# Turning half of the attention probabilities by a DRAM round trip and VectorE instead of TensorE

## The chip, the cores and the metric

The kernel runs on one core of one Trainium2 chip, in one launch. The metric is the device time of that launch in microseconds (us). Before the change the median of three runs is 933.17 us (932.65 to 934.37).

## The reference, cut to what matters

One "macaron" block over a sequence of 2048 tokens with 1024 features: half a feed-forward layer, an attention layer, and the other half of the feed-forward layer, each added to its input.

```python
x = x + 0.5 * ffn(layernorm(x))
x = x + attention(layernorm(x))
x = x + 0.5 * ffn(layernorm(x))
```

The attention works in blocks of 128 tokens. A convolution over three tokens gives q, k and v (256 features each), and these are projected to 16 heads of 64. The part around the change is this, for each block `b` and head `h`:

```python
scores = einsum('bqhe,bkhe->bhqk', qh * scale, kh)
scores = where(causal, scores, -1e9)
p = softmax(scores, axis=-1)
o = einsum('bhqk,bkhe->bqhe', p, vh)
o = einsum('bqhe,hed->bqd', o, wo) + bo
out = o @ proj_w + proj_b
```

TensorE contracts over partitions. The scores come out with the queries on the partitions, and the product with `vh` contracts over the keys. So each 128 x 128 matrix `p` has to be turned in between. There are 16 blocks and 16 heads, 256 such matrices.

## The kernel before

The first feed-forward layer, the convolution (done as a fast convolution of eight products, line 585) and the second feed-forward layer (main products at line 311) are not touched. The change lies in the attention, from about 418 us to 785 us of the profile.

**Turns.** The tokens are split into 4 groups of 512 (4 blocks), numbered g = 0 to 3. The heads are taken two at a time (a "head pair" hp, its two heads j = 0 and 1), and two head pairs make one turn, r = 0 to 3. So there are 16 turns, i = 4 g + r, from 0 to 15. One turn deals with four tiles of probabilities, each 128 queries x 4 blocks x 128 keys (128 x 512 fp32, 256 KB), in a pool of four buffers: the copy that fills a tile in one turn has to wait until the same tile of the turn before has been read.

**TensorE's order is written out by hand** (`turn`, L1227, inside `manual_schedule`). In turn i TensorE does:

- `stage_qk` of turn i (pq, L870), the q and k projections
- `stage_wo` of turn i - 2 (acc, L1133)
- `stage_transpose` of turn i - 1 (pt, L1103): 16 transposes of 128 x 128, four to a tile
- `stage_scores` of turn i (sc, L1056)
- `stage_values` of turn i - 1 (ao, L1116), first for its first head pair, then for its second
- in turns with r = 0, i > 0, `stage_v` (pv, L870); in turns with r = 1, g > 0, `stage_proj` of the group before (pp, L1196). In turn 1, `stage_v` of group 0 stands ahead of the transposes.

So turns with r = 2 and 3 are short and turns with r = 0 and 1 are long, and a tile's softmax has the time from the scores of its turn to the transposes of the next. After turn 15 comes a hand-written tail, which mixes the end of the attention with the start of the second feed-forward layer (`Second`, L371).

**The softmax of a turn** (`stage_scores`, L1048): ScalarE copies the four score tiles from PSUM (L1065, kept in program order), GpSimd masks each (L1070), VectorE takes the row maxima (L1081), ScalarE does 16 exponentials with their sums (L1086), all after the last copy, and VectorE inverts the sums (L1093) and scales the tile (L1094, the "division"). `stage_transpose` then has TensorE turn a tile into PSUM, and ScalarE (j = 0, L1106) or VectorE (j = 1, L1108) copy it out as `pT`.

**The order on the other engines** is that of a planner, which sorts by priority, and is fixed when the program is built. Every engine's queue is worked off in order. That holds for the queue of SyncE (SP), which issues nearly all loads and stores, and for GpSimd's (POOL), which issues the accumulating DMAs between its other work: an instruction that waits holds up all that stand behind it.

**What else stands in these queues**, and is named later:

- `tokens_of` (L896): q and k of a later group, `x<-qkv`, four loads of 256 KB on SP, with their sums on GpSimd and VectorE (L851 to L854)
- `signs` (L1212): weights of the second feed-forward layer, `raw`, 512 KB each on SP, turned into signs by ScalarE (L1215)
- `load_residual` (L1146): the residual rows, `xr<-x` (L1149), four loads of 512 KB on SP, and on GpSimd's queue four accumulating DMAs that add `proj_b` to them (L1150), each waiting for its load
- `row_statistics` (L1154): in turns with r = 1 and 2, ScalarE's normalized rows `xp` (L1174) and their stores by quarters, `xq<-xp` (L1184), 16 of 128 KB for each group
- in the tail, `Second.load` (L378): `xl<-xq`, 512 KB each on SP (L380), and `Second.transpose` (L382), where VectorE turns them in 32 x 32 blocks (STREAM_TRANSPOSE, L387).

In the tail the load of `xl` for the first row tile, its two VectorE transposes and the four accumulating DMAs of the last group stand ahead of the maxima and masks of turn 15 in their queues, before the change and after it.

Of the kernel before, what the change touches and what calls it, by code (L numbers as in the profile page):

```python
# [9 lines left out]
F32 = mybir.dt.float32  # L10
# [3 lines left out]
ALU = mybir.AluOpType  # L14
AX = mybir.AxisListType
PSUM = bass.MemoryType.PSUM

P = 128
NB = 512
# [5 lines left out]
def kernel(  # L25
# [22 lines left out]
    nc = tc.nc  # L48
# [10 lines left out]
    BPG = NB // P  # L59
    NH2 = D // NB  # L60
    QC = 32
    QSCALE = 1.0 / (DH**0.5)

    def pool(stack, name, bufs, **kw):
        return stack.enter_context(tc.tile_pool(name=name, bufs=bufs, reuse_waits="tile", **kw))
# [4 lines left out]
    spill = pool(ctx, "spill", 1, space=DRAM)  # L70
# [4 lines left out]
    def bank(kind, shape, name):  # L75
        return banks[kind].tile(shape, F32, name=name, tag=kind)
# [26 lines left out]
    def pin(ins):  # L103

        return tc.keep_in_program_order(ins)
# [878 lines left out]
    with ExitStack() as ph:  # L984
        ow = pool(ph, "ow", 1)
        ap4 = pool(ph, "ap4", 4)
# [8 lines left out]
        prs, pTs, oTs, accs, qks, ended, stored, exps, maxima, masked, turned, divided = ({} for _ in range(12))  # L995
# [49 lines left out]
        def held(ins):  # L1045
            return tc.issue_after(ins.ins) if ins else ExitStack()

        def stage_scores(g, r, mask_behind=None, maxima_behind=None):  # L1048
            ps = []
            for hp, kind in zip((2 * r, 2 * r + 1), ("mm", "tr")):  # L1050
                qh, kh = qks.pop((g, hp))

                sc = [bank(kind, [P, BPG, P], f"sc_{g}_{hp}_{j}") for j in range(2)]
                for b in range(BPG):
                    for j in range(2):
                        nc.tensor.matmul(  # L1056
                            sc[j][:, b, :],
                            lhsT=qh[ts(j, DH), ts(b, P)],
                            rhs=kh[ts(j, DH), ts(b, P)],
                            start=True,  # L1060
                            stop=True,
                        )
                prs[g, hp] = [ap4.tile([P, BPG, P], F32, name=f"p_{g}_{hp}_{j}", tag="p") for j in range(2)]
                for p, acc in zip(prs[g, hp], sc):
                    copied = pin(nc.scalar.copy(p, acc)).ins  # L1065
                    ps.append(p)

            for n, p in enumerate(ps):
                with held(mask_behind):
                    masked[g, r] = nc.gpsimd.affine_select(  # L1070
                        out=p,
                        in_=p,
                        pattern=[[0, BPG], [-1, P]],
                        compare_op=ALU.is_ge,
                        fill=NEG_INF,
                        base=0,
                        channel_multiplier=1,
                    )
                nmax = small.tile([P, BPG], F32, name=f"anm_{g}_{r}_{n}", tag="anmax")
                with held(maxima_behind):  # L1080
                    ins = nc.vector.tensor_reduce(nmax, p, AX.X, ALU.max, negate=True)  # L1081
                maxima.setdefault((g, r), ins)
                asum = small.tile([P, BPG], F32, name=f"asum_{g}_{r}_{n}", tag="asum")
                with tc.issue_after(copied):
                    for b in range(BPG):
                        exps[g, r] = nc.scalar.activation(  # L1086
                            p[:, b, :],
                            p[:, b, :],
                            AF.Exp,
                            bias=nmax[:, b : b + 1],  # L1090
                            accum_out=asum[:, b : b + 1],
                        )
                nc.vector.reciprocal(asum, asum)  # L1093
                divided[g, r] = nc.vector.tensor_tensor(  # L1094
                    p, p, asum.unsqueeze(2).broadcast_to([P, BPG, P]), ALU.mult
                )

        def stage_transpose(g, hp, kind):
            pTs[g, hp] = []
            for j, p in enumerate(prs.pop((g, hp))):  # L1100
                pt = bank(kind, [P, BPG, P], f"pt_{g}_{hp}_{j}")
                for b in range(BPG):
                    nc.tensor.transpose(pt[:, b, :], p[:, b, :], ident)  # L1103
                pT = ap4.tile([P, BPG, P], F32, name=f"pT_{g}_{hp}_{j}", tag="pT")
                if j == 0:
                    nc.scalar.copy(pT, pt)  # L1106
                else:
                    turned[g, hp] = nc.vector.tensor_copy(pT, pt)  # L1108
                pTs[g, hp].append(pT)
# [108 lines left out]
        pairs = [(g, r) for g in range(NG) for r in range(NP)]  # L1218
# [8 lines left out]
        def turn(g, r, values):  # L1227
# [13 lines left out]
            if i == 1:  # L1241
                stage_v(0)
            two(stage_wo, i - 2)
            two(stage_transpose, i - 1, "sm", "tr")
            stage_scores(g, r)
            if values:
                two(stage_values, i - 1)
# [15 lines left out]
        with tc.manual_schedule(engines={mybir.EngineType.PE}):  # L1263
# [7 lines left out]
            g, r = pairs[-1]  # L1271
# [16 lines left out]
            for t in range(2):  # L1288
                load_rows2(t)
            two(stage_wo, LAST - 3)  # L1290
            two(stage_transpose, LAST - 2, "sm", "tr")
            with tc.issue_after(turned[g, NHP - 3].ins), tc.high_priority(offset=400):
                ffn.transpose(0)
            ffn.load(2)
            stage_scores(g, r, stored[g], ffn.turned)
            with tc.issue_after(masked[g, r].ins):
                for t in range(2):
# [3 lines left out]
            two(stage_wo, LAST - 2)  # L1301
            ffn.gate(0)
            stage_transpose(g, NHP - 2, "sm")
            with tc.issue_after(divided[g, r].ins):
                ffn.transpose(1)
# [75 lines left out]
```

## Time and profile before

| | |
|---|---|
| median of the three runs | 933.17 us |
| the profiled execution's own time | 932.75 us |
| its span (first to last instruction) | 930.9 us |
| TensorE (PE) busy | 908.7 us, 98% of the span |
| VectorE (DVE) busy | 673.3 us, 72% |
| ScalarE (ACT) busy | 451.0 us, 48% |
| GpSimd (POOL) busy | 234.8 us, 25% |
| PE transposes of p (pt, L1103) | 256, from 446.5 to 761.6 us |
| from the first score copy (L1065) of turns 4, 5, 6 and 7 to that of the next turn | 28.00, 28.99, 16.57, 15.85 us |

"Busy" does not say that an engine bounds a stage: matmuls are pipelined, and shares are averages. What sets the time is read from the chain of work that ended last and from the timelines of the single turns. A time line gives start and duration in us from the start of the span, engine, source line, operation, output and inputs, number of instructions, and in brackets the idle time before and what ended it. SPq is SyncE's queue of DMA issues. The first copies of turns 4 to 8 start at 496.84, 524.84, 553.83, 570.40 and 586.25 us.

### The profile page before, as it was taken

The page shows a single profiled execution, that of the slowest core. Times are in us where ns is not written, and L with a number is a line of the kernel's source. Part 1 is how long each engine was busy: PE and PEld are TensorE (multiplying, and loading weights), DVE is VectorE, ACT ScalarE, POOL GpSimd, SP SyncE. Part 2 cuts the span into 40 slices and gives each one's busy share as a digit, 9 for nine tenths or more (in the row PEclk, how much of TensorE's full clock was granted, in tenths as well). Part 3 has the DMA queues.
Part 4 walks back from the last instruction along what each step waited for, and adds up shares of the span by engine and source line. Part 5 has one row for each costly group of instructions (what it writes and reads, how often), then busy time and mean ns, then how long its engine had stood idle before and what let it go on. Part 6 is the DMA issues. An engine that isn't in the chain of part 4 may idle for free.

```text
span 930.9 us, 14379 instructions
## 1 busy us (share of the span) xinstructions
PE 908.7 (98%) x5112; PEld 647.9 (70%) x5112; DVE 673.3 (72%) x1353; ACT 451.0 (48%) x1231; POOL 234.8 (25%) x331
## 2 busy tenths in 40 slices
PE   6999999999999999999999999999999999999997
PEld 4778888886666666666775677667765765777775
DVE  5889887689978786657786668576757566866663
ACT  5676666431111111117787758666766752423230
POOL 2554454320001011101141123112412222443341
PEclk9999999999999999999999999999999999999999
DMA  9776663499576765445460149015702593997853
GB/s 350 172 197 191 183 192 137 153 297 348 178 223 176 202 189 128 89 160 181 148 139 10 46 147 283 25 47 168 193 1 92 189 263 130 313 271 217 246 159 113
DMA packets 51063, 161.64 MB, mean 174 GB/s; under 512 B 6376, under 2 KB 15592, under 8 KB 49072
## 3 DMA queue, kind: packets, MB, share of 16 engines
q1 hardware_dynamic: 39568, 114.69, 35.0%
q0 software_dynamic: 10688, 38.02, 20.9%
q10 hardware_dynamic: 736, 8.02, 2.3%
q8 instruction: 40, 0.66, 0.3%
q14 instruction: 31, 0.25, 0.1%
HBM read 97.69 MB, written 46.24 MB: 155 GB/s over the span
## 4 chain that ended last, share of the span: by engine, by line
PE 81%; DVE 6%; ACT 4%; DMA 3%; issue 3%; POOL 2%; SPq 0%; POOLq 0%; ACTq 0%; DVEq 0%
PE cv L585 23%; PE pm_f L311 20%; PE pq L870 8%; PE pp L1196 6%; PE pv L870 5%; PE acc L1133 4%; PE sc L1056 3%; PE ao L1116 3%; PE pt L1103 3%; DMA x<-in_x_dram 2%; PE lgp_f L228 2%; PE is_f L272 1%; ACT p L1086 1%; PE tr_f L220 1%; DVE st_f L167 1%
## 5 line engine op out<-in xcount | busy, mean ns | idle before, releaser
L311 PE MATMUL pm_f<-sw,y_f 128*128 128x512 f32 x1024 | 258.1, 403 | 0.6 <-ACT y_f L285 0.4
L311 PEld LDWEIGHTS pm_f<-sw,y_f 128*128 128x128 f32 x1024 | 187.0, 190 | 41.9 <-ACT y_f L285 0.8
L585 PE MATMUL cv<-v,u 128*128 128x342 f32 x576 | 166.0, 450 | 0.0
L585 PEld LDWEIGHTS cv<-v,u 128*128 128x128 f32 x576 | 109.0, 189 | 56.8
L286 POOL TENSOR_TENSOR y_f<-xnT_f,y_f 128x512 fp32r<-128x512 f32 x63 | 79.9, 1283 | 111.4 <-ACT y_f L285 111.4
L1086 ACT ACTIVATE p<-p,anm 128x128 f32<-128x128 f32 x256 | 99.9, 400 | 0.4 <-DVE anm L1081 0.4
L1070 POOL TENSOR_SCALAR_AFFINE_SELECT p<-p 128x512 f32<-128x512 f32 x64 | 39.3, 654 | 220.6 <-ACT p L1065 220.6
L602 ACT ACTIVATE m<-cv 128x342 f32<-128x342 f32 x42 | 19.2, 457 | 156.2 <-PE cv L585 154.1
L323 DVE TENSOR_TENSOR pm_f<-pm_f,os_f 128x512 f32<-128x512 f32 x64 | 44.7, 698 | 52.7 <-PE pm_f L311 52.4
L1081 DVE TENSOR_REDUCE anm<-p 128x4 f32<-128x512 f32 x64 | 40.2, 679 | 25.9 <-POOL p L1070 25.6
L585 PE MATMUL cv<-v,g 128*128 128x342 f32 (+2 forms) x224 | 57.1, 415 | 0.9 <-DVE v L507 0.9
L1133 PE MATMUL acc<-oT,wo_sb 128*128 128x512 f32 x128 | 57.9, 594 | 0.0
L1196 PE MATMUL pp<-pw_sb,o2T 128*128 128x512 f32 x128 | 56.6, 597 | 0.3 <-DVE xr L1204 0.3
L585 PEld LDWEIGHTS cv<-v,g 128*128 128x128 f32 x224 | 39.7, 190 | 17.6 <-DVE v L507 1.3
L1086 ACT ACTIVATION_READ_ACCUMULATOR p<-p,anm 128x1 f32 x256 | 51.0, 199 | 0.0
L1108 DVE COPY pT<-pt 128x512 f32<-128x512 f32 x32 | 22.1, 691 | 38.4 <-PE pt L1103 38.3
L297 ACT ACTIVATE os_f<-po_f 128x512 f32<-128x512 f32 x64 | 34.8, 595 | 24.3 <-PE is_f L272 14.1
L1094 DVE TENSOR_TENSOR p<-p,asum 128x512 f32<-128x512 f32 x64 | 44.9, 701 | 1.3
L1196 PEld LDWEIGHTS pp<-pw_sb,o2T 128*128 128x128 f32 x128 | 23.7, 190 | 30.1 <-issue 25.0
L573 DVE SCALAR_TENSOR_TENSOR u<-g,u 128x1024 f32<-128x1024 f32 x18 | 22.0, 1224 | 29.0 <-PE cv L585 13.2
L285 ACT CAST y_f<-xnT_f 128x512 fp32r<-128x512 f32 x64 | 37.5, 625 | 11.2 <-DVE xnT_f L283 11.2
L283 DVE TENSOR_TENSOR xnT_f<-xnT_f,is_f 128x512 f32<-128x512 f32 x64 | 40.9, 679 | 2.3 <-PE is_f L272 2.3
(190 smaller groups left out, 1645.5 us busy)
## 6 DMA issues: line engine op xcount, KB each, us to landing
g<-in_conv_w_dram SPq DMA_DIRECT2D x28, 512.0 KB, 4.9
u<-in_conv_w_dram POOLq DMA_DIRECT2D x24, 512.0 KB, 6.2
x<-in_x_dram SPq DMA_DIRECT2D x16, 512.0 KB, 4.6
raw<-in_weight_t_dram SPq DMA_DIRECT2D x16, 512.0 KB, 8.8
x<-hbias POOLq DMA_DIRECT2D x16, 512.0 KB, 5.5
x<-x SPq DMA_DIRECT2D x16, 512.0 KB, 4.2
xr<-x SPq DMA_DIRECT2D x16, 512.0 KB, 5.2
xr<-in_proj_b_dram POOLq DMA_DIRECT2D x16, 512.0 KB, 9.1
```

Source lines behind the costliest of these rows:

```text
L283: self.scaled = nc.vector.tensor_tensor(y, y, sc, ALU.mult)
L286: self.lowered = lows[h].tensor_tensor(yl, y, yh.bitcast(F32), ALU.subtract)
L311: ins = nc.tensor.matmul(pms[h], lhsT=y[:, n, c, :], rhs=self.sw[:, c, ts(h, NB)], start=(c == 0 and n == 0), stop=(c == DC - 1 and n == 1),)
L323: nc.vector.tensor_tensor(pms[h], pms[h], o, ALU.mult)
L585: nc.tensor.matmul(accs[w, k][:, lo:hi], lhsT=uk[:, c, :], rhs=V[k][:, c, lo:hi], start=(c == 0), stop=(c == DC - 1),)
L870: nc.tensor.matmul(leave.sums[sums], lhsT=rows[a][:, u, :], rhs=cols[b], start=n in (0, 1, 3), stop=True, skip_group_check=True,)
L1070: masked[g, r] = nc.gpsimd.affine_select(out=p, in_=p, pattern=[[0, BPG], [-1, P]], compare_op=ALU.is_ge, fill=NEG_INF, base=0, channel_mu ...
L1081: ins = nc.vector.tensor_reduce(nmax, p, AX.X, ALU.max, negate=True)
L1086: exps[g, r] = nc.scalar.activation(p[:, b, :], p[:, b, :], AF.Exp, bias=nmax[:, b : b + 1], accum_out=asum[:, b : b + 1],)
L1094: divided[g, r] = nc.vector.tensor_tensor(p, p, asum.unsqueeze(2).broadcast_to([P, BPG, P]), ALU.mult)
L1133: nc.tensor.matmul(accs[g][m], lhsT=wo_sb[:, hp, ts(m, P)], rhs=oT, start=(hp == 0), stop=(hp == NHP - 1),)
L1196: nc.tensor.matmul(pp, lhsT=o2T[:, m, ts(b, P)], rhs=pw_sb[:, m, ts(h, NB)], start=(m == 0), stop=(m == WC - 1),)
```

## The change

For every turn but the last, the tiles of the second head (j = 1) of both head pairs no longer go through TensorE, 30 tiles of the 64. Their scores are copied and kept with the keys in quarters, (quarter, block, key in the quarter). They take the lead in the softmax. After its division such a tile is stored to DRAM in four pieces, one for each quarter of the partitions, so that the quarter of the queries and the quarter of the keys change places, and is loaded back into the same tile. Then VectorE turns it in 32 x 32 blocks straight into `pT`. The planner may put the transposes only behind the last division of their turn. The tiles with j = 0, and all of turn 15, are as before.

```diff
+        def by_quarters(p):
+            return p.rearrange("p q (b k) -> p q b k", b=BPG)
+
+        def exchange(p, name):
+            there = spill.tile([P, NB], F32, name=name)
+            to = there.rearrange("(q b) c -> b q c", q=4)
+            for k in range(4):
+                nc.sync.dma_start(out=to[:, :, ts(k, P)], in_=p[ts(k, QC)])
+            nc.sync.dma_start(out=p, in_=there.rearrange("p (q c) -> p q c", q=4))
...
+            turned_on_vector = (g, r) != pairs[-1]
...
-                for p, acc in zip(prs[g, hp], sc):
+                for j in (1, 0) if turned_on_vector else (0, 1):
+                    p, acc = prs[g, hp][j], sc[j]
+                    quarters_of = turned_on_vector and j == 1
+                    if quarters_of:
+                        p, acc = by_quarters(p), acc.rearrange("p b (q k) -> p q b k", q=4)
                     copied = pin(nc.scalar.copy(p, acc)).ins
-                    ps.append(p)
-
-            for n, p in enumerate(ps):
+                    ps.append((quarters_of, hp, p))
+
+            for n, (quarters_of, hp, p) in enumerate(sorted(ps, key=lambda x: -x[0])):
+                if quarters_of:
+                    rows_of, width = p.rearrange("p q b k -> p b q k"), [4, QC]
+                    pattern = [[-QC, 4], [0, BPG], [-1, QC]]
+                else:
+                    rows_of, width = p, [P]
+                    pattern = [[0, BPG], [-1, P]]
...
+                if quarters_of:
+                    exchange(prs[g, hp][1], f"exchange_{g}_{hp}")
...
             for j, p in enumerate(prs.pop((g, hp))):
+                if j == 1 and (g, hp // 2) != pairs[-1]:
+                    pT = ap4.tile([P, BPG, P], F32, name=f"pT_{g}_{hp}_{j}", tag="pT")
+                    with tc.issue_after(divided[g, hp // 2].ins):
+                        turned[g, hp] = nc.vector.transpose(
+                            pT.rearrange("p b (t k) -> p t b k", t=4), by_quarters(p)
+                        )
+                    pTs[g, hp].append(pT)
+                    continue
```

Mask, maxima, exponentials and division of these tiles do the same arithmetic on the other layout.

More of the change, by code (lines that the diff above doesn't have):

```diff
@@ L1072, in stage_scores @@
                         in_=p,
-                        pattern=[[0, BPG], [-1, P]],
+                        pattern=pattern,
                         compare_op=ALU.is_ge,
@@ L1080, in stage_scores @@
                 with held(maxima_behind):
-                    ins = nc.vector.tensor_reduce(nmax, p, AX.X, ALU.max, negate=True)
+                    ins = nc.vector.tensor_reduce(
+                        nmax, rows_of, AX.XY if quarters_of else AX.X, ALU.max, negate=True
+                    )
                 maxima.setdefault((g, r), ins)
@@ L1086, in stage_scores @@
                         exps[g, r] = nc.scalar.activation(
-                            p[:, b, :],
-                            p[:, b, :],
+                            rows_of[:, b],
+                            rows_of[:, b],
                             AF.Exp,
@@ L1093, in stage_scores @@
                 nc.vector.reciprocal(asum, asum)
+                each = asum.unsqueeze(2).unsqueeze(3) if quarters_of else asum.unsqueeze(2)
                 divided[g, r] = nc.vector.tensor_tensor(
-                    p, p, asum.unsqueeze(2).broadcast_to([P, BPG, P]), ALU.mult
+                    rows_of, rows_of, each.broadcast_to([P, BPG, *width]), ALU.mult
                 )
+                if quarters_of:
+                    exchange(prs[g, hp][1], f"exchange_{g}_{hp}")
         def stage_transpose(g, hp, kind):
@@ L1100, in stage_transpose @@
             for j, p in enumerate(prs.pop((g, hp))):
+                if j == 1 and (g, hp // 2) != pairs[-1]:
[3 more added lines that the diff above has]
+                            pT.rearrange("p b (t k) -> p t b k", t=4), by_quarters(p)
+                        )
+                    pTs[g, hp].append(pT)
+                    continue
                 pt = bank(kind, [P, BPG, P], f"pt_{g}_{hp}_{j}")
```

## The prediction

> **What bounds it now.** I read the chain of work that ended last first (part 4 of the page), then single turns of the attention.
>
> ```profile
> PE 81%; DVE 6%; ACT 4%; DMA 3%; issue 3%; POOL 2%; SPq 0%; POOLq 0%; ACTq 0%; DVEq 0%
> ```
>
> The same chain in order of time, for turns 7 and 8:
>
> ```profile
> 583.34 1.75 PE pt L1103 x16
> 585.08 1.99 PE sc L1056 x32
> 587.07 1.90 PE ao L1116 x32
> 588.97 12.23 PE pv L870 x28
> 601.86 6.06 PE pq L870 x26
> 607.91 3.43 PE acc L1133 x8
> 611.35 1.75 PE pt L1103 x16
> ```
>
> TensorE is passed from stage to stage without a gap, so a removed transpose is time saved, as long as what takes its place arrives. 16 transposes take 1.75 us, 0.109 each.
>
> I now count time t from a turn's first score copy (L1065). A timeline shows how little air a short turn has: VectorE's divisions in turn 7 (first copy 570.40).
>
> ```profile
> 576.38 0.68 DVE L1094 TENSOR_TENSOR p<-p,asum 128x512 f32<-128x512 f32 x1
> 577.18 0.69 DVE L1094 TENSOR_TENSOR p<-p,asum 128x512 f32<-128x512 f32 x1
> 579.62 0.69 DVE L1094 TENSOR_TENSOR p<-p,asum 128x512 f32<-128x512 f32 x1
> 581.86 0.69 DVE L1094 TENSOR_TENSOR p<-p,asum 128x512 f32<-128x512 f32 x1
> ```
>
> The four divisions end at t = 6.7, 7.5, 9.9 and 12.2; TensorE reaches the transposes at t = 12.8 and the values at 16.7. In turn 6 the last division ends at 568.46, t = 14.6, and TensorE waits inside its transposes (0.44 us for `asum`, 0.18 for `p`). There the softmax sets the pace, and a shorter TensorE wins nothing.
>
> **What goes and what comes.** Per turn for turns 0 to 14: 8 of 16 transposes go, 8 x 0.109 = 0.875 us of TensorE. Two VectorE copies out of PSUM (L1108, 0.69 us) go, two VectorE transposes of 128x512 come:
>
> ```profile
> L387 DVE STREAM_TRANSPOSE xnT_f<-xl_f 128x512 f32<-128x512 f32 x4 | 2.6, 685 | 0.0
> ```
>
> That is equal work for VectorE. Mask, maxima, exponentials and divisions change their strides only. The nearest row is the strided `xp` (L1174, 1.24 us for 1024 elements) against the plain `sw` (L1215, 1.04 us): 0 to 19%, on 8 exponentials of 0.385 us at most 0.6 us a turn, and I take 0. The gain is bounded by 15 x 0.875 = 13.1 us.
>
> Per turn SP gets 10 more DMAs: for the first tile A four stores of 64 KB and a load of 256 KB, for the second tile B the same. The trace of before has none of them; the nearest rows are
>
> ```profile
> xq<-xp SPq DMA_DIRECT2D x12, 128.0 KB, 2.2
> vx<-qkv SPq DMA_DIRECT2D x2, 256.0 KB, 3.2
> ```
>
> with extremes of 1.9 to 8.1 us for the store and 3.1 to 4.4 for the load (9.8 for the crowded 256 KB loads `x<-qkv`). An issue takes SP 0.30 to 0.44 us. I take 2.0, 3.1 and 0.4. [...]
>
> **The round trip in a short turn.** The built order puts SP's issues as A0 to A3, B0 to B2, load A, B3, load B. A load must wait until its stores have landed. With A divided at t = 6.4 and B at about 8: A's stores issue until 8.1; B0 to B2 until 9.3; load A at 9.7, landed 12.9; B3 at 10.2, landed 12.3; load B at 12.4, landed 15.5; VectorE turns B by 16.4. The values of the second head pair want B at 16.7 + 0.95 - 0.87 = 16.8. So the plain round trip just fits, by 0.4 us. It fits where nothing stands between on SP, and in most short turns something does:
>
> - *Turn 1.* Load B stands behind `raw`, which waits until ScalarE has done the signs of the raw rows before (t = 13.1). Load B goes at 13.4 and is behind 1 MB; B is turned at about 17.9, 1.2 us late. The next turn's copy into B's buffer is late too, so its softmax is, and there it runs into VectorE's token sums (L851 to L854, 3 us). Turns 1 and 2 together: +0.3 against before instead of -1.75. Turn 3: -0.1.
> - *Turns 6 and 10.* A's stores stand behind four `xq` stores, which wait for a ScalarE row (L1174) that now lies inside the exponentials, ending at t = 7.2. A's stores go from 8.9 to 10.5, load A at 12.5, load B at 15.5 behind 768 KB of tokens or 1 MB of `raw`; B is turned at about 19.8, wanted at 18.5. The late copy puts off turn 7's (11's) softmax by 2 us. Turns 6 and 7 together +0.4, 10 and 11 the same.
> - *Turn 14.* The same `xq` wait, but the order on ScalarE is better than before in the copies: -0.25.
>
> Sum of the short turns: 0.3 - 0.1 + 0.4 + 0.4 - 0.25 = **+0.8** (bounds: -7.0 if all eight keep their saving, +8 if each is 1 us late on top).
>
> *Long turns* (0, 4, 5, 8, 9, 12, 13) have 12 us more: 7 x -0.875 = -6.1. Back from that: 0.5 at turns 4, 8 and 12, where B of the short turn before is late by that much; and 1.3 at turn 12, where GpSimd's fourth mask stands behind an accumulating DMA, which waits for `xr` now loaded only after the exchange; VectorE waits for that mask (t = 8.3) with the additions of `vh` behind it, which TensorE needs at 8.4 and gets at 9.7. **-3.3** (bounds -6.1 to 0).
>
> **The tail.** This is the largest term. Before, SP issued the residual loads and the first `xl` early in turn 14 (first copy 732.30), and GpSimd and VectorE were through with them in time:
>
> ```profile
> 736.83 1.90 SPq L1149 DMA_DIRECT2D xr<-x  x4
> 738.78 1.27 SPq L380 DMA_DIRECT2D xl_f<-xq  x2
> ```
> ```profile
> 741.91 0.91 POOL L1150 DMA_DIRECT2D xr<-in_proj_b_dram  x1 [5.73 <-DMA xr<-x]
> 743.14 0.87 POOL L1150 DMA_DIRECT2D xr<-in_proj_b_dram  x1 [0.32 <-issue]
> 744.40 0.86 POOL L1150 DMA_DIRECT2D xr<-in_proj_b_dram  x1 [0.39 <-issue]
> 745.64 0.86 POOL L1150 DMA_DIRECT2D xr<-in_proj_b_dram  x1 [0.38 <-issue]
> 748.53 2.40 POOL L1070 TENSOR_SCALAR_AFFINE_SELECT p<-p 128x512 f32<-128x512 f32 x4 [2.02 <-ACT p L1065]
> ```
>
> In the built order of the changed kernel these loads stand behind turn 14's load B. So `xr` goes at t = 15.6 instead of 4.5. GpSimd's first accumulating DMA came 5.1 us after that issue, and the four take 4.6: 15.6 + 5.1 + 4.6 = 25.3, and only then come the masks of turn 15 (0.65): 25.9. `xl` goes at 17.5, landed 7.6 later (its row) at 25.1; its two VectorE transposes (1.29) stand ahead of turn 15's maxima: 26.4. Before, the first maximum of turn 15 started at 749.19, t = 16.9. **+9.5 us**, for both queues give the same time. Behind the maxima stand the additions of `oT`, for which TensorE's acc waits, and the exponentials, which were on the chain (752.01, 4.73 us). Nothing else is there for TensorE: the whole tail moves. Bounds: `xr` at t = 13 to 18 gives +7 to +12; 0 if the tail had slack, for which I see no sign.
>
> The clock: a break of 1.5 us at 755.5 was followed by
>
> ```profile
> 758.00:759.00 1.00, 0.63 (x6) 0.63 (x8) 1.00 (x3) 0.00 (x0) 0.36 (x1) 0.52 1.04 270
> 759.00:760.00 1.00, 1.00 (x12) 0.94 (x8) 0.53 (x1) 0.00 (x0) 0.50 (x1) 0.50 1.02 250
> 760.00:761.00 1.00, 1.00 (x6) 0.73 (x5) 0.62 (x1) 0.00 (x0) 0.00 (x0) 0.50 1.15 234
> ```
>
> (the third number from the right is the granted clock): some 3.7 us at half speed, about 1.8 us lost. A break of 9 us earlier costs the same once, while the exponentials run anyway, and may spare the second: -1.8 to +1.8, I take 0. [...]
>
> **Sum.** -3.3 + 0.8 + 9.5 = +7.0 on the profiled execution's own 932.75 (span 930.9 and 1.85 around it): 939.8. The median, 933.17, lies 0.42 above that run: **940.2 us**.
>
> **Rivals.**
>
> 1. *The round trip fits everywhere* (other side). If B is turned by t = 16.8 in the short turns too, all 15 turns keep 0.875: -13.1, and the tail costs its lower 7 to 9.5: -6 to -3.6, 927 to 929.6. For it: the plain sum fits by 0.4 us. Against: `raw` and `xq` waits on SP. It decides at that 16.8. Chance 0.13.
> 2. *The tail has slack*, or `xr` and `xl` land sooner: the tail costs 3, the turns as above: +0.5, 933.7. Against: both queues give the same delay. 0.11.
> 3. *The exchange becomes the loop of the short turns.* The copy of the next turn waits for B's buffer; with stores or loads 2 to 3 us slower than I take, every short turn runs at 18 us instead of 15.8: 8 x 2 = +16 more, 956. For it: extremes of 8.1 and 9.8 in the rows. 0.10.
>
> That it doesn't do what it says is excluded by the built order: 30 transposes on VectorE, 150 DMAs on SP, 120 transposes fewer on TensorE.
>
> My forecast has 0.66. Its own range is 935.2 to 947 (tail 7 to 12, turns -5 to +2). The range for 8 in 10 is 930 to 948, with part of 1 and all of 2. 0.2% (1.9 us) is about what a measurement of this kernel can tell from no change: faster 0.13, within it 0.11, slower 0.76.
>
> **What will show it.** Right: `xr` issued by SP some 11 us later against turn 14's first copy; a TensorE gap of 8 to 10 us after turn 14's values, with VectorE waiting for `xl` or GpSimd's mask; long turns shorter by 0.9; pairs of short turns no shorter. Wrong: that gap under 4 us, or the short turns at 14.8 (rival 1) or 18 (rival 3).

## The result, and the profile after

The changed kernel takes 979.14 us (median; 976.98 to 980.55) against 933.17 before: **slower by 4.9%**, ratio 1.0489 (95% interval 1.0463 to 1.0515). The profiled execution took 977.81 us, its span is 976.0 us: 45.1 more than before. The forecast was 940.2 (930 to 948): the sign was right, the size was not.

The chain of work that ended last, shares by engine, from the page:

```profile
PE 56%; issue 17%; DMA 10%; DVE 8%; ACT 5%; SPq 2%; POOL 1%; POOLq 0%; ACTq 0%; DVEq 0%
```

TensorE's share has fallen from 81% to 56%, and DMA's has risen from 3% to 10%. The shares are rough: `issue`, stretches of up to 34 us in which the chain names no releaser, went from 3% to 17%. What TensorE waits for (us in total, times, longest):

```profile
PE ao L1153 <- DVE pT L1133: 15.9, 8, 3.6
PE pq L870 <- DVE qk L1017: 12.5, 3, 6.4
PE acc L1170 <- DVE oT L1162: 12.3, 1, 12.3
```

Three waits that hardly were there before (0.4, 0.6 and nothing): for the tiles that VectorE turns, above all those of the short turns; for the q and k projections of the long turns 4 and 8; and one break of 12.3 us in the tail. The new work itself costs what its rows promised, first VectorE's transposes in the attention, then the DMAs (KB each, median us to landing):

```profile
L1133 DVE STREAM_TRANSPOSE pT<-p 128x512 f32<-128x512 f32 x30 | 20.5, 700 | 21.7 <-DMA p<-exchange 21.6
```
```profile
exchange<-p SPq DMA_DIRECT2D x120, 64.0 KB, 1.8
p<-exchange SPq DMA_DIRECT2D x30, 256.0 KB, 3.0
```

700 ns stands against 691 for the copies that went, and 1.8 and 3.0 us against the 2.0 and 3.1 of the forecast. A median hides the few that matter.

**Where the 45.1 us arose.** An interval is the time from a turn's first score copy to that of the next turn; the tail is what follows turn 15's first copy (good to 0.1, like the spans). The last five columns say how far each kernel's profile is from before; the experiments are told below.

| interval | before | changed | no trip | six long | short only | 3, 7, 11 |
|---|---|---|---|---|---|---|
| up to turn 0 | 426.66 | +1.13 | +0.71 | +0.39 | +0.78 | +0.47 |
| 0 (long) | 22.92 | -0.61 | -0.62 | -0.63 | +0.02 | +0.01 |
| 1 | 15.62 | -1.04 | -1.04 | +0.74 | -1.03 | 0.00 |
| 2 | 16.01 | +4.36 | -0.15 | 0.00 | +6.66 | +0.02 |
| 3 | 15.63 | +1.09 | -1.04 | +0.01 | +0.67 | -1.05 |
| 4 (long) | 28.00 | **+9.55** | -0.81 | -0.70 | +3.34 | +2.12 |
| 5 (long) | 28.99 | -0.83 | -0.83 | -0.85 | +0.01 | 0.00 |
| 6 | 16.57 | +0.66 | +0.16 | -0.46 | -0.01 | -0.19 |
| 7 | 15.85 | +3.56 | -1.30 | -0.25 | +0.73 | -1.27 |
| 8 (long) | 28.01 | **+8.79** | -0.81 | -0.62 | +1.92 | +1.89 |
| 9 (long) | 28.99 | -0.64 | -0.84 | -0.85 | +0.02 | 0.00 |
| 10 | 16.36 | +0.88 | +0.37 | -0.24 | +0.19 | +0.02 |
| 11 | 15.87 | +4.14 | -1.31 | -0.28 | +3.24 | -1.29 |
| 12 (long) | 27.83 | +0.95 | -0.87 | -0.90 | +1.65 | +1.65 |
| 13 (long) | 28.99 | -0.83 | -0.84 | +0.04 | +0.01 | 0.00 |
| 14 | 15.57 | -0.10 | -0.28 | 0.00 | -0.46 | 0.00 |
| tail | 183.03 | **+14.04** | +0.80 | +2.50 | +10.96 | -0.78 |

For the changed kernel: start 1.1, long turns 16.4, short turns 13.6, tail 14.0; together 45.1. Three places are read below.

**Turn 4** (first copy 501.77), SP's queue:

```profile
501.81 1.86 SPq L1186 DMA_DIRECT2D xr<-x  x4
508.96 6.47 SPq L1058 DMA_DIRECT2D exchange<-p  x7
522.25 0.34 SPq L1059 DMA_DIRECT2D p<-exchange  x1
522.64 1.40 SPq L1058 DMA_DIRECT2D exchange<-p  x1
525.49 0.34 SPq L1059 DMA_DIRECT2D p<-exchange  x1
525.88 0.90 SPq L956 DMA_DIRECT2D vx<-qkv  x2
```

The residual rows `xr` went in turns 0 and 1 before (those of turn 8 in turn 6); now they stand behind the exchange of turn 3 and so go at the start of turn 4: 2 MB, and GpSimd's accumulating DMAs on the same 2 MB. The stores come next and land late (median 9.8 us in this stretch). It is the accumulating DMAs that they are late with, and not the loads: the fourth of them (GpSimd's line) went at 511.47, when the last `xr` had landed, and three stores that went after that took 9.8 us in the median all the same (second line, from 511.6 to 515):

```profile
511.47 0.86 POOL L1187 DMA_DIRECT2D xr<-in_proj_b_dram  x1 [0.99 <-DMA xr<-x]
```
```profile
exchange<-p SPq DMA_DIRECT2D x3, 64.0 KB, 9.8
```

That last accumulating DMA landed at 521.74, and these three stores at 522.30, 522.47 and 522.64. So load A, which must wait for A's stores, goes 13.3 us after the first of them, and behind load B stands `vx`, at t = 24.1 in place of 15.0. VectorE's next instruction waits for it:

```profile
529.08 0.42 DVE L839 TENSOR_TENSOR vs<-vx 128x256 f32<-128x256 f32 x1 [7.82 <-DMA vx<-qkv]
```

and behind these sums, in VectorE's queue, stands the evacuation of q and k (L1017), which TensorE needs:

```profile
530.60 1.22 PE L870 MATMUL pq<-t,wq_sb 128*128 128x256 f32 x2 [6.42 <-DVE qk L1017]
```

How full the DMA engines were, in stretches of 4 us (second number from the right: their busy share; third: the granted clock), the changed kernel first, then before in the same part of turn 4:

```profile
508.00:512.00 4.00, 4.00 (x11) 1.82 (x10) 3.03 (x6) 3.95 (x17) 2.24 (x3) 1.00 1.10 254
512.00:516.00 4.00, 4.00 (x11) 1.79 (x10) 2.36 (x6) 3.15 (x13) 0.33 (x1) 1.00 1.03 207
```
```profile
504.00:508.00 4.00, 4.00 (x11) 1.78 (x10) 1.89 (x5) 4.00 (x16) 0.00 (x0) 1.00 0.01 2
```

They were idle in this stretch before, and full after.

With this the 9.55 us of turn 4 add up (an estimate): some 1.8 for turn 3's late B (TensorE waits 1.38 us for it, and by experiment 7 a wait of 1.2 makes a turn 1.65 longer), 6.4 for `vx`, and 2.1 because TensorE then ran 4.3 us at half the granted clock (0.50); less the 0.87 saved, 9.5. In turn 8 the same terms are 1.2, 5.5 and 2.9, together 8.8.

**Turns 6 and 7**: load B of turn 6 goes just ahead of the last token load and 1 MB of `raw`, with 768 KB of tokens before it:

```profile
583.82 0.32 SPq L1059 DMA_DIRECT2D p<-exchange  x1
584.18 0.43 SPq L827 DMA_DIRECT2D x<-qkv  x1
584.95 0.87 SPq L1251 DMA_DIRECT2D raw<-in_weight_t_dram  x2
```

It lands 5.3 us later; VectorE turns B, and TensorE has waited for it:

```profile
589.13 0.71 DVE L1133 STREAM_TRANSPOSE pT<-p 128x512 f32<-128x512 f32 x1 [2.31 <-DMA p<-exchange]
...
589.89 1.97 PE L1153 MATMUL ao<-pT,vh 128*64 128x128 f32 x14 [3.14 <-DVE pT L1133]
```

In VectorE's queue this transpose stands between the first and the second maximum of turn 7, and ScalarE's fourth copy of turn 7 waits for its buffer (3.59 us). So turn 7's softmax is late as a whole, and its own exchange after it.

**The tail**: `xr` and `xl` at t = 16.1 and 18.0 of turn 14 (763.46) in place of 4.5 and 6.5; the first `xl` lets VectorE go 11.8 us after its issue, and TensorE stands still until VectorE has got past it:

```profile
779.60 1.87 SPq L1186 DMA_DIRECT2D xr<-x  x4
781.50 1.09 SPq L380 DMA_DIRECT2D xl_f<-xq  x2
```
```profile
793.33 1.31 DVE L387 STREAM_TRANSPOSE xnT_f<-xl_f 128x512 f32<-128x512 f32 x2 [10.84 <-DMA xl_f<-xq]
```
```profile
795.91 6.26 PE L1170 MATMUL acc<-oT,wo_sb 128*128 128x512 f32 x8 [12.28 <-DVE oT L1162]
```

### The profile page after: what moved, and what is told of

It reads as the page before. It is cut to its first block, busy times and chain, and to the rows that moved or that the text cites. A ratio compares the mean times of both kernels' runs of the same rounds, so it can differ in the third digit from the quotient of the medians.

```text
span 976.0 us, 14568 instructions
## 1 busy us (share of the span) xinstructions
PE 909.7 (93%) x4992; PEld 643.0 (66%) x4992; DVE 673.3 (69%) x1353; ACT 452.7 (46%) x1231; POOL 238.1 (24%) x331
## 4 chain that ended last, share of the span: by engine, by line
PE 56%; issue 17%; DMA 10%; DVE 8%; ACT 5%; SPq 2%; POOL 1%; POOLq 0%; ACTq 0%; DVEq 0%
PE pm_f L311 22%; PE cv L585 19%; DMA exchange<-p 3%; PE pp L1233 3%; PE pv L870 3%; DMA x<-in_x_dram 2%; ACT p L1112 2%; PE pq L870 2%; DMA p<-exchange 2%; PE lgp_f L228 2%; PE is_f L272 1%; PE acc L1170 1%; PE tr_f L220 1%; DMA xl_f<-xq 1%; SPq L1058 1%
## 5 line engine op out<-in xcount | busy, mean ns | idle before, releaser
L1112 ACT ACTIVATE p<-p,anm 128x128 f32<-128x128 f32 x256 | 99.6, 395 | 12.9 <-DVE anm L1105 12.3
L1094 POOL TENSOR_SCALAR_AFFINE_SELECT p<-p 128x512 f32<-128x512 f32 x64 | 42.2, 702 | 231.8 <-ACT p L1083 227.9
L1170 PE MATMUL acc<-oT,wo_sb 128*128 128x512 f32 x128 | 63.7, 643 | 12.3 <-DVE oT L1162 12.3
L1170 PEld LDWEIGHTS acc<-oT,wo_sb 128*128 128x128 f32 x128 | 26.5, 209 | 39.9 <-issue 25.6
L1153 PE MATMUL ao<-pT,vh 128*64 128x128 f32 x512 | 37.3, 286 | 16.4 <-DVE pT L1133 15.9
L1013 ACT ACTIVATE qk<-pq,sbq 128x256 f32<-128x256 f32 x64 | 30.1, 471 | 37.8 <-PE pq L870 37.5
L1083 ACT COPY p<-sc 128x512 f32<-128x512 f32 x64 | 33.8, 595 | 27.3 <-DVE pT L1133 19.6
L1153 PEld LDWEIGHTS ao<-pT,vh 128*64 128x64 f32 x512 | 30.7, 141 | 21.4 <-DVE pT L1133 17.9
```

The costliest lines, as they stand in the source:

```text
L1094: masked[g, r] = nc.gpsimd.affine_select(out=p, in_=p, pattern=pattern, compare_op=ALU.is_ge, fill=NEG_INF, base=0, channel_multiplier=1,)
L1112: exps[g, r] = nc.scalar.activation(rows_of[:, b], rows_of[:, b], AF.Exp, bias=nmax[:, b : b + 1], accum_out=asum[:, b : b + 1],)
L1153: nc.tensor.matmul(po[ts(j, DH), b, :], lhsT=vh[:, b, ds((hp % NP) * P + j * DH, DH)], rhs=pT[j][:, b, :], start=True, stop=True,)
L1170: nc.tensor.matmul(accs[g][m], lhsT=wo_sb[:, hp, ts(m, P)], rhs=oT, start=(hp == 0), stop=(hp == NHP - 1),)
```

## The experiments

My theory from this profile: the engines' work and the round trip as such are cheap; what costs is the place of the exchange in SP's queue, next to transfers of one or several MB. The rivals: the new layout and VectorE's transposes cost more than the rows say; or every exchange costs its 3 us (46 us over 15 turns), wherever it is.

**1. The exchange left out, everything else kept**

```diff
-                if quarters_of:
+                if False:
                     exchange(prs[g, hp][1], f"exchange_{g}_{hp}")
```

> Leaves out the stores to DRAM and the loads back (150 DMAs); VectorE's transposes read the tile as divided, so the second head's matrices are turned wrongly. The new layout, the VectorE transposes and the 120 missing TensorE transposes stay. Theory (the cost is the queue and the transfers, not the engines' work): the 13.1 us of TensorE come through as far as the short turns' softmax lets them, 920 to 926 us. Rival (strided softmax and VectorE transposes cost more than the PSUM copies did): above 931.

924.96 us, ratio 0.9917 (0.9902 to 0.9931). The 150 DMAs therefore cost 54 us, and all the rest of the change gains 8. Long turns keep 0.81 to 0.87 each (0.62 in turn 0), as counted; the short ones -1.31 to +0.37, where the softmax sets the pace. The first rival is out.

**2. Only the seven long turns**

```diff
-            turned_on_vector = (g, r) != pairs[-1]
+            turned_on_vector = g * NP + r in (0, 4, 5, 8, 9, 12, 13)
```

(and the same condition in `stage_transpose`; likewise in all experiments that choose turns)

> The exchange only in the seven turns that have the 12 us of v or out-projection products behind their values (0, 4, 5, 8, 9, 12, 13); the other nine as before. The residual loads then have no exchange ahead of them in turns 3, 7, 11 and 14. Theory (what hurts is the place of the bulk loads and the short turns): 7 x 0.87 saved, 926 to 929 us. Rival (every exchange costs about 3 us wherever it is, 46 us over 15 turns): 950 or more.

931.36 us, 0.9983 (0.9973 to 0.9993), less than expected. Six turns gave their 0.85 to 0.88 and turn 0 0.64, so the second rival is out. But turn 1 lost 0.74, turn 14 1.06 and the tail 3.27, without an exchange there. Turn 1's loss is not settled. For turn 14 and the tail, ScalarE's last `xp` had moved from between the copies of turn 14 into its exponentials, its `xq` stores held SP up, and `xr` went at t = 9.3.

**3. The residual loads ahead of the exchange** of turns 3, 7, 11 and 14 (and the first two `xl` loads ahead of that of 14)

```diff
-            if r == 0 and g > 0:
-                load_residual(g - 1)
+            if r == 0 and g > 0:
+                add_to_residual(g - 1)
+            if r == NP - 1 or i == LAST - 2:
+                load_residual(g)
```

(`load_residual` split into its loads and its accumulating DMAs)

> All 15 turns with the exchange; only the residual loads xr of a group (and the first two xl loads of the second feed-forward layer) are put ahead of the exchange of turns 3, 7, 11 and 14 in SP's queue. Theory (these loads pushed behind the exchange cost turns 4 and 8 some 9 us each and the tail 14): 979 - 18 - 14 = 947, 943 to 953 with turn 14's exchange now behind 3 MB. Rival (the DMA engines are simply too full for the extra traffic, whatever the order): 965 to 980.

998.85 us, 1.0708 (1.0682 to 1.0734): slower still; neither theory had that. Now the exchange waits. Turns 4, 8 and 12 are 8.6, 12.1 and 8.4 us longer than before, the tail 24.4. In turn 14 the stores stand behind 3 MB and the accumulating DMAs, and land after 15.4 us in the median, TensorE waits 18.6 us for the tile. DMA issues, then TensorE's line:

```profile
exchange<-p SPq DMA_DIRECT2D x8, 64.0 KB, 15.4
```
```profile
810.55 1.98 PE L1153 MATMUL ao<-pT,vh 128*64 128x128 f32 x16 [18.56 <-DVE pT L1133]
```

In turns 3, 7 and 11 the loads had landed when the stores went, and beside the accumulating DMAs alone these took 4.3 to 10.1 us. So it is not the order alone: the two do not fit side by side in one short turn, and whichever goes second is late.

**4. No exchange in turn 14**

```diff
-            turned_on_vector = (g, r) != pairs[-1]
+            turned_on_vector = g * NP + r < 14
```

> The exchange in turns 0 to 13; turn 14 goes through TensorE as before. Theory (the tail's 14 us come from xr and xl standing behind turn 14's exchange): 979 - 14 + 0.9 = 966 us. Rival (the tail is late through the DMA traffic left over from earlier, or through the masks): 974 or more.

971.05 us, 1.0412 (1.0395 to 1.0429), between the two expectations. Turn 14 and tail together are still 5.8 us longer than before, of the 13.9: `xr` goes at t = 9.3 here too, for the reason seen in experiment 2. So about 8 us of the tail belong to turn 14's exchange, the rest to `xp`'s new place.

**5. Six long turns**, without turn 13

```diff
-            turned_on_vector = (g, r) != pairs[-1]
+            turned_on_vector = g * NP + r in (0, 4, 5, 8, 9, 12)
```

> The exchange only in the long turns 0, 4, 5, 8, 9 and 12 (not 13). In the run with seven long turns the intervals of 4, 5, 8, 9, 12 and 13 were each 0.85 to 0.88 us shorter, but the tail was 3.3 and turn 14 1.1 us longer: there ScalarE's last row xp had moved behind the copies of turn 14, its xq stores hold up SP, and xr went at t = 9.3 instead of 4.5. Without turn 13's exchange xp stands as before. Theory (the tail follows xr): 931.4 - 4.3 + 0.9 = 928, 927 to 929. Rival (the tail is longer through DMA traffic or the layout, not through that order): 931 to 933.

928.65 us, 0.9956 (0.9942 to 0.9969): **faster than before**, by 0.4%. `xp` and `xr` (t = 4.53) are back in place and turn 14 takes 15.57 as before. The profile's tail is still 2.5 longer, but that lies in the second feed-forward layer (two waits of 0.8 and 0.9 us of its routing for VectorE, among others); why, is not settled. The first maximum of turn 15 comes as early as before, and the profiled execution, 930.58 us, is the slowest of the five.

**6. Only the eight short turns**

```diff
-            turned_on_vector = (g, r) != pairs[-1]
+            turned_on_vector = g * NP + r in (1, 2, 3, 6, 7, 10, 11, 14)
```

> The reverse: the exchange only in the short turns 1, 2, 3, 6, 7, 10, 11 and 14. xr is still pushed from turns 3, 7 and 11 into turns 4, 8 and 12, but finds no exchange there. Theory (turns 4 and 8 lose 9 us each because the exchange's stores stand behind xr and its accumulating DMAs, then vx behind the exchange): turns 4 and 8 as before, short turns and tail as in the full change: 933 + 13.6 + 14 = 960, 957 to 964. Rival (the late xr itself, or vx behind it, costs turns 4 and 8): 975 to 982.

962.58 us, 1.0320 (1.0290 to 1.0349). Turns 4 and 8, with `xr` late but no exchange of their own, lose 3.3 and 1.9, not 9: the theory's side. No store of this run took more than 3.6 us, though a load B beside `raw` in turn 1 took 5.7.

**7. Only turns 3, 7 and 11**

```diff
-            turned_on_vector = (g, r) != pairs[-1]
+            turned_on_vector = g * NP + r in (3, 7, 11)
```

> The exchange only in turns 3, 7 and 11, the short turns without raw, tokens or xq stores in their queue. Theory (the plain round trip of a short turn just fits, and the full change's 3.6 to 4.4 us in turns 2, 7 and 11 come from the bulk loads beside the exchange of turns 1, 2, 6 and 10): the second tile is turned at t = 16.5 to 17.5, wanted at 16.8; -0.87 in intervals 3, 7 and 11 and up to +0.7 in 4, 8 and 12: 931 to 933. Rival (the round trip of two tiles is too long for any short turn, 3 us late each time): 938 to 943. xr is pushed into turns 4, 8 and 12 here too; if that alone costs 9 us each, 950 or more.

936.01 us, 1.0032 (1.0019 to 1.0045): dearer than expected, between the theory (up to 933) and the first rival (from 938); the second rival (from 950) is out. The three turns save 1.05 to 1.29, and the next ones lose 1.65 to 2.12. Load B goes at t = 13.35, without neighbours its store lands after 1.8 us and its load after 2.6, but VectorE takes up two maxima of the next turn first (starting at 497.62, turn 3's first copy is at 481.7):

```profile
498.81 0.70 DVE L1137 STREAM_TRANSPOSE pT<-p 128x512 f32<-128x512 f32 x1
```
```profile
499.57 1.09 PE L1157 MATMUL ao<-pT,vh 128*64 128x128 f32 x14 [1.23 <-DVE pT L1137]
```

B is done at t = 17.8, 1.2 us after TensorE wanted it. The first rival's late round trip is there, but 1.2 us late and not 3.

**8 and 9. The kernel before, with `xr` made late**, by a small store on SP that waits for the last division of the turn; first in turn 14, then in turns 3, 7 and 11

```diff
+                    hold = spill.tile([1, NB], F32, name="hold")
+                    pin(nc.sync.dma_start(out=hold, in_=prs[NG - 1, 2 * NP - 3][1][0:1]))
                     load_residual(NG - 1)
```
```diff
+                hold = spill.tile([1, NB], F32, name=f"hold_{g}")
+                pin(nc.sync.dma_start(out=hold, in_=prs[g - 1, 2 * NP - 1][1][0:1]))
                 load_residual(g - 1)
```

> The kernel before, without any exchange; only the last group's xr loads and the first two xl loads are made late: ahead of them on SP stands a 2 KB store of a row of turn 14's last divided tile, so xr goes at about t = 15 instead of 4.5. Theory (the tail's loss is xr and xl being late, about one for one beyond what GpSimd and VectorE have to spare): over the runs xr at 6.5, 9.3, 14.6 and 16.1 gave +0.5, +4.3 to 5.8, +10.5 and +13.9; so 10 to 12 us, 943 to 945. Rival (a good part of the 13.9 is the traffic of the exchange itself): 936 to 939.

> The kernel before with the xr loads of the first three groups made late in the same way, into turns 4, 8 and 12; the tail as before. Theory (late xr does no harm in a long turn that has no exchange): within 0 to 2 us of before, 932 to 935. Rival (late xr or vx behind it costs turns 4 and 8 by itself): 945 or more.

940.67 us, 1.0088 (1.0062 to 1.0113), and 933.78 us, 1.0009 (0.9999 to 1.0020). The first lies between its two expectations: `xr` went at t = 13.5, earlier than I meant. The tail is 8.4 longer with no exchange anywhere, so most of the tail's loss is `xr` and `xl` being late. The first maximum of turn 15 tells it best; t from turn 14's first copy, the loss is of turn 14 and tail together:

| | `xr` issued | first maximum of turn 15 | loss |
|---|---|---|---|
| before | 4.5 | 16.9 | 0 |
| seven long turns (2) | 9.3 | 20.2 | 4.3 |
| not turn 14 (4) | 9.3 | 20.9 | 5.8 |
| before, `xr` late (8) | 13.5 | 24.5 | 8.4 |
| short only (6) | 14.6 | 27.7 | 10.5 |
| changed | 16.1 | 31.1 | 13.9 |

The loss follows the maximum to within about 2 us. That is also how far turn 14 and tail scatter where the maximum is in its old place (-0.8 to +2.5 in experiments 5, 7, 9, 10 and 12).

In the second one `xr` went at t = 12.5 to 13.9 of turns 3, 7 and 11, some 3 us ahead of its time in the changed kernel; its accumulating DMAs ran in turn 4 from t = 0.6, the last landing at 16.2. Alone they do next to nothing to a long turn. Turns 4 and 8 in the four combinations:

| | `xr` early | `xr` late, its accumulating DMAs in turns 4 and 8 |
|---|---|---|
| no exchange there | 28.00, 28.01 (before) | -0.04, +0.18 (9); with an exchange in 3 and 7: +2.12, +1.89 (7) and +3.34, +1.92 (6) |
| exchange there | -0.70, -0.62 (5) | +9.55, +8.79 (changed) |

In 6 and 7 some 1.65 is the late B of turn 3 or 7, as in their turn 12; the rest, at most 1.7, is late `xr` and `vx`. An exchange alone gains 0.6 to 0.7. So of the 9 us the meeting of the two in one turn costs some 7.

**10 and 11. Both heads exchanged**, in five of the six long turns, and in three

```diff
-                    quarters_of = turned_on_vector and j == 1
+                    quarters_of = by_vector(g, r, j)
```

(`by_vector` is true for j = 0 too in turns 4, 5, 8, 9, 12, or in 5, 9, 12)

> The six long turns as in the run with 928.65 us, and in 4, 5, 8, 9 and 12 the tiles of both heads are exchanged: 20 DMAs a turn in place of 10, all 16 TensorE transposes gone, and ScalarE's copies out of PSUM with them. Theory (in a long turn without other bulk loads the exchange has room to spare; at one head each the second tile was turned at t = 21 to 22, wanted at 28): another 5 x 0.87 saved, 924.3, 923 to 926. Rival (twice the DMAs push the last load and vx behind it past what TensorE needs in turns 4 and 8): no gain there or 1 to 3 us lost each, 927 to 932.

> The same with both heads only in turns 5, 9 and 12, where no vx load stands behind the exchange. Theory: another 3 x 0.87, 926.0, 925 to 927. If vx is what limits turns 4 and 8, this one is the faster of the two.

934.23 us, 1.0017 (1.0006 to 1.0027), and 935.23 us, 1.0026 (1.0015 to 1.0037). Both expectations failed, and `vx` was not the reason: in the first run turns 4, 8 and 12 gained 1.8 to 1.9 each, but in both turn 5 took 33.5 us and 32.1 us (28.14 with one head), turn 9 32.7 and 32.5. There load D (of the turn's fourth tile) stands in SP's queue ahead of an `xq` store; ScalarE's third row waits for that store's buffer, and the copies of turn 6 stand behind the rows:

```profile
551.42 1.24 ACT L1215 ACTIVATE xp<-xr,sh_f,rs_f 128x1024 f32<-128x1024 f32 x1 [3.91 <-DMA xq<-xp]
```

**12. Both heads in 4, 8 and 12, one in 0, 5 and 9**

```diff
-                    quarters_of = turned_on_vector and j == 1
+                    quarters_of = i in (0, 4, 5, 8, 9, 12) and (j == 1 or i in (4, 8, 12))
```

(`i` is `g * NP + r`; the same condition wherever a tile is turned)

> Both heads exchanged in turns 4, 8 and 12, the second head alone in 0, 5 and 9. In the runs with both heads, turns 4, 8 and 12 were 1.9, 1.9 and 1.8 us shorter than before (0.7, 0.6 and 0.9 with one head), but turns 5 and 9 longer by 3.1 to 4.5, where the fourth tile's load on SP holds up an xq store, that a row xp on ScalarE, and that the copies of turns 6 and 10. Theory (it is the queue of stores, not the exchange): 928.65 - 3.4 = 925.3, 924 to 927. Rival (more exchange costs elsewhere whatever the turn): 928 or more.

925.81 us, 0.9919 (0.9904 to 0.9935): **the best version**, 7.1 us under the kernel before. Turns 4, 8 and 12: -1.92, -1.93, -1.78; turns 5 and 9: -0.89 each.

## Why the prediction was wrong

By its own steps; times are of the profiled executions.

- **TensorE's 0.875 us a turn, VectorE's equal work, no cost of the strides: right.** Experiment 1 keeps 0.81 to 0.87 in the long turns; an exponential takes 395 ns (400 before), a division 702 (701).
- **The plain round trip "fits by 0.4 us": wrong by 1.6.** Experiment 7 has it alone: load B goes at 13.35 (I had 12.4), and VectorE's queue has two maxima ahead of B, so B is done at 17.8 (16.4). TensorE waits 1.2.
- **The short turns, +0.8: mis-sized, 13.6.** The mechanisms named are there (`raw` ahead of load B in turn 1, `xq` ahead of A's stores in 6 and 10). Turn 1's B was turned at 18.9, a microsecond after what I said. But turns 1 and 2 cost 3.3 instead of 0.3, 6 and 7 4.2 instead of 0.4, 10 and 11 5.0. Load B of turn 6 landed 5.3 us after its issue, beside 2 MB, and B was turned from 21.7 on, not by 19.8; and I charged a late B once, while it delays the next turn's maxima and its fourth copy, hence its whole softmax and its exchange.
- **The long turns, -3.3 (bounds -6.1 to 0): this step failed**, they cost 16.4. I took their 12 us of products as room for any exchange, and priced the moved `xr` loads only by GpSimd's mask in turn 12. There the sum came out (+0.95; I had -0.87 + 0.5 + 1.3 = +0.9), but by luck: TensorE's only break is 1.4 us for turn 11's B, which thus costs 1.8 and not 0.5, and the fourth mask, which did come behind an accumulating DMA (VectorE waits 1.4 us for it), costs TensorE nothing instead of 1.3. In turns 4 and 8 the accumulating DMAs on the same rows are in flight when the stores come, and `vx`, which of the turns with moved `xr` only these two have, stands behind load B. I had the order of SP's queue and did not ask who waits for `vx`, nor what accumulating DMAs do to a store of 64 KB.
- **The tail, +9.5: right in mechanism, mis-sized, 14.0.** `xr` went at 16.1 (15.6), the masks started at 27.0 (25.3), but `xl` took 11.8 us instead of the 7.6 of its row, so VectorE's transposes started at 29.9 and not at 25.1. Why 11.8, with `xl` 7.7 in experiment 8, is not settled. The `xq` wait of turn 14 was in my 15.6 as part of the exchange's path; experiment 4 shows that without an exchange in turn 14 it puts `xr` at 9.3, with turn 14 and tail 5.8 longer.
- **The clock, 0: within its bounds.** The first maximum is 14.2 late, the tail 14.0 longer. After its break TensorE ran 5.2 us at half the granted clock (0.50), against 3.4 us in all before (I had read 3.7).
- The 1.1 us ahead of turn 0 lie in a part that is not changed (among them a wait for gate rows, 3.9 instead of 2.8).

Of the rivals, the first two fell. The third came nearest in size (956), and the copies did wait for B's buffer (19.6 us in all), but there is no uniform loop of 18 us: short turns took 14.6 to 20.4, and a clean short turn (experiment 7) takes 14.6 and gives 1.65 to 2.1 back in the next.

The cause is thus shown for the tail (experiments 4, 8), for turns 4 and 8 (5, 6, 9: late `xr` and an exchange in one turn) and for the DMAs as a whole (1). That the stores are late through the accumulating DMAs is read from the traces (turn 4, 9.8 us in the median, and experiment 3, 4.3 to 10.1 us with no loads beside them); no run left these DMAs out. For the pairs of short turns the traces show what B waits for; no run took the tokens or `raw` away.

## What to carry to other kernels

A store of 64 KB took 1.8 us here in the median, but 9.8 and 15.4 us in the turns where it met accumulating DMAs: before adding a round trip, write down which bulk loads, and above all which accumulating DMAs, are in flight or will be pushed next to it, and who waits for the loads that now stand behind it. Where some places in a schedule have room and others have not, apply the change to those places alone: 15 turns cost 46 us, the six good ones, three of them with double the work, gain 7. Moving the big loads ahead only exchanged the victims (experiment 3).

## What the runs showed of the hardware

- A store of 64 KB landed after 1.8 us in the median (120 stores of the changed kernel), after 9.8 in turn 4 of the changed kernel, beside the accumulating DMAs, and after 15.4 in turn 14 of experiment 3. Over all runs, a store of the exchange took more than 4.2 us only beside accumulating DMAs (changed, experiments 3 and 4), and then 4.3 to 17.2; the others, some beside up to 1 MB of loads pushed around them, took at most 4.2. In the changed kernel each late store landed 0.2 to 1.0 us after an accumulating DMA. A plain load next to them was less late: `vx` in turn 4 of experiment 6 took 3.8 and 5.1. Why a store lands so late beside them, no run shows.
- The DMA engines counted as full (share 1.03 to 1.10) at 207 to 254 GB/s in turn 4 with the accumulating DMAs in flight, and at some 410 GB/s with plain loads alone (experiment 8, from 750 to 751 us).
- Some breaks of TensorE were followed by half the granted clock, short ones too: after breaks of 1.5 us (before, at 755.5), 3.1 us (turn 7) and 6.4 us (turn 4) it fell to 0.50, some 2.6 to 3.9 us after they began, and TensorE then worked 3.0 to 4.3 us at half the clock, some 1.5 to 2.1 us of work lost on top of the break. Not each short break did it: after one of 1.8 us (changed, at 487.1) the clock stayed at 1.00.
